# Layer 0 of a two-layer hybrid attention block: filler units four at a time with other VectorE steps behind each, all output projections first, and row sums one group later

## The chip, the cores and the metric

The kernel runs on one core of a Trainium2 chip. The metric is device time in microseconds (us), the median of three runs. Times quoted from the profile come from one profiled execution.

## What is computed

Two layers work on x of shape (2, 512, 64, 32), which is 2 batches of 512 channels and 2048 tokens, all in fp32. The change lies almost wholly in layer 0, whose reference, shortened, is:

```python
emb = get_embeddings(B, H, W, 32, 32)            # 32 frequency + 32 time channels
qk_hs = concatenate([hidden_states, emb], axis=1)   # 576 channels for q and k
q = qk_hs @ Wq
k = qk_hs @ Wk
v = v_hs @ Wv                                    # 512 channels for v
scores = einsum('bhqd,bhkd->bhqk', q, k) / sqrt(64)   # 8 heads of 64
attn = softmax(scores)
o = einsum('bhqk,bhkd->bhqd', attn, v)
x = o @ Wout + bout + hidden_states
```

Layer 1 takes a layer norm of this result per token, then attention by landmarks (256 landmarks, a pseudo-inverse by iteration), and then a second layer norm and a linear map whose weights are unpacked from 4-bit codes ("the feed-forward map"). The change touches the layer norm that stands at the head of layer 1, the place where the map's weights are unpacked, and one small function of layer 1.

## The kernel before

**Engines and order.** The instruction order on TensorE (PE), VectorE (DVE), ScalarE (ACT) and GpSimd (POOL) is the order in which the program issues them: these queues are scheduled by hand (L2070). Loads go out on SyncE's queue (SP). Stores of `x1_d` and `xh_d` go out on POOL's queue. A waiting instruction therefore holds up everything behind it on its engine.

**Layer 0's heads.** Heads are handled in pairs, `Heads0(b, hp)`: two batches with four pairs each, eight pairs in all, numbered n = 0 to 7 here and called "heads" below. For each, `attention0` (L1028) makes 64 steps (t, c): four blocks t of 512 queries, and for each 16 blocks c of 128 keys. Steps go in groups of two (GROUP = 2), at i = 0, 2, ... 64. For one group the program issues, in this order:

- the scores of its two steps on PE (L1040), in 64x64 tiles, into PSUM banks named "sc" (two of them), each followed by an exponential on ACT (L1048) into one of six SBUF tiles "p";
- two additions of p into `acc` on VectorE (L1058);
- the values of the group before it on PE (L1070), again in 64x64 tiles, into the banks av0 and av1 (one each); on the last key block of t, a copy of av0 on ACT (L1076) and an addition of av1 on VectorE (L1077) set the two banks free;
- some filler units (below);
- when a block t has ended, `sums` (L1080 and on): two row-sum matmuls of `acc` with ones on PE (`rs`, L1084), a reciprocal on VectorE (L1088) and the multiplication of the output by it on POOL (L1089).

**Filler units.** Between groups, PE works on generators. `advance(gens, n)` (L775) takes up to n units from a list of them, oldest first; a generator that yields GAP is passed over for this time. The units of the next head are: the embedding part of q (`fp`, a matmul of 96 columns L863, a VectorE copy `ft` L865, and an addition over 128x2048 on POOL, `e`, L867), four projections of q (four 128x512 matmuls each, L879, and the addition of `e` on VectorE, L882), the same for k, four units of v (16 matmuls each, L924, and an ACT copy L931), and last the reductions `big` on VectorE (2 x L912, L914). That is 15 units. In head 4 (b = 1, hp = 0) the list also holds `finish0_units` of batch 0: for each of four token blocks, a load of x, four output projections (`yp`, L939, with an addition on VectorE, L946), a store to `x1_d`, and the layer norm of the block, `norm0_steps`: partial sums on VectorE (`part`, L957 and L958), a mean matmul (L961), a subtraction (L962), two squares on ACT and two additions (L965 to L971), a variance matmul (L974), a square root on ACT, a reciprocal (L991), two multiplications (POOL L993, VectorE L994), and a store of `xh_d` (L995). Here the norm of one block is interleaved with the projections of the next. All of fp, pp, vp, yp, mean, var, and rs take turns in two PSUM banks ("pp").

**The steps beside.** `feed_forward_map` (L1113) unpacks the map's weights in 46 VectorE steps, most of them two pairs of operations (L1135, L1136), and ends in four PE units (`mp`). In heads 0 to 3 one step is taken in groups 1, 3 and 5 of every eight.

**How many fillers at a time.** With `due` as the share of the head's units that should have been made by group i, `attention0` takes two or three units when at least two are due; in head 4 (`every`) it takes one or two in every group. At the end of a head all units that are left of the next head are made.

**Start.** The first head's q, k and v are made before the first `attention0`. The weights and the embedding are loaded over SP, ACT's and POOL's queues (L803 to L815).

**`attend`** (layer 1, L1243) computes the scores of two landmark heads into the two halves of one PSUM tile `scs` (L1255) and exponentiates each into X on ACT (L1262), for pairs i = 0 to 2 of each batch; for i = 3 each half has a bank of its own.

Of the kernel before, what the change touches and what calls it, by code (L numbers as in the profile page):

```python
# [17 lines left out]
B, C, H, W = 2, 512, 64, 32  # L18
S = H * W
KC = C // P  # L20
# [641 lines left out]
def fast_path(  # L662
# [62 lines left out]
    def chunked(ap):  # L725
        return ap.rearrange("(k p) n -> p k n", p=P)
# [4 lines left out]
    def scores_bank(name):  # L731
        return ps.tile([P, 2, 512], F32, tag="sc", name=name)
# [18 lines left out]
    def block_of(pool, tag, name):  # L751
        return pool.tile([P, KC, TB], F32, tag=tag, name=name)
# [40 lines left out]
    def gap(n=1):  # L793
        for _ in range(n):
            yield GAP
# [5 lines left out]


    emb_sb = wpool0.tile([64, H + W], F32, name="emb_f")  # L803
    nc.vector.memset(emb_sb, 0.0)
    w_sb = {kind: wpool0.tile([P, KC, C], F32, name=f"w{kind}_f") for kind in "qk"}
    we = {kind: wpool0.tile([64, C], F32, name=f"we{kind}_f") for kind in "qk"}

    def load_w0(kind, cols, queue=nc.sync):
        w = {"q": wq0, "k": wk0}[kind]
        nc.sync.dma_start(w_sb[kind][:, :, cols], chunked(w[:C, cols]))  # L810
        queue.dma_start(we[kind][:, cols], w[C:, cols])

    nc.gpsimd.dma_start(emb_sb[:32, :H], freq)
    nc.gpsimd.dma_start(emb_sb[32:, H:], time)
    load_w0("q", slice(0, P), nc.scalar)  # L815

    def load_x(src, b, name, first=0, n=NTB):
        tiles = []
# [21 lines left out]
    class Heads0:  # L840
# [13 lines left out]
        def embedded_and_projected(self, kind):  # L854

            cols, xbs = self.cols, self.xbs
            if kind == "q":
                self.q = qopool.tile([P, S], F32, tag="qo", name=f"q_{self.name}")

            def embedded(kind):  # L860

                fp = bank(f"fp_{kind}_{self.name}")
                nc.tensor.matmul(fp[:, : H + W], lhsT=we[kind][:, cols], rhs=emb_sb, start=True, stop=True)  # L863
                ft = wpool0.tile([P, H + W], F32, tag="ft", name=f"ft_{kind}_{self.name}", bufs=2)
                nc.vector.tensor_copy(ft, fp[:, : H + W])  # L865
                e = wpool0.tile([P, H, W], F32, tag="e", name=f"e_{kind}_{self.name}")
                nc.gpsimd.tensor_tensor(  # L867
                    e,
                    ft[:, :H].unsqueeze(2).to_broadcast([P, H, W]),
                    ft[:, H:].unsqueeze(1).to_broadcast([P, H, W]),  # L870
                    ALU.add,
                )
                return e.rearrange("p h w -> p (h w)")

            def project(kind, dst, e, t):
                toks = slice(t * TB, (t + 1) * TB)
                pp = bank(f"pp_{kind}_{self.name}_{t}")
                for k in range(KC):
                    nc.tensor.matmul(  # L879
                        pp, lhsT=w_sb[kind][:, k, cols], rhs=xbs[t][:, k, :], start=k == 0, stop=k == KC - 1  # L880
                    )
                nc.vector.tensor_tensor(dst[:, toks], pp, e[:, toks], ALU.add)  # L882

            dst = self.q if kind == "q" else self.k
            e = embedded(kind)
            yield
            yield GAP
            for t in range(NTB):
                project(kind, dst, e, t)
                yield  # L890
# [104 lines left out]
        nc.gpsimd.dma_start(chunked(xh_d[b])[:, :, toks], xn)  # L995
        yield

    N_FINISH0 = NTB * (KC + 2)

    def finish0_units(b, oTs, outs_done):  # L1000
        last = None
        for t in range(NTB):
            xb = block_of(lpool, "xr", f"xr_f0_{b}_{t}")
            nc.sync.dma_start(xb, chunked(x[b])[:, :, t * TB : (t + 1) * TB])
            yield from gap()

            for m, _ in enumerate(out0_units(b, t, xb, oTs)):
                if last and m == 0:
                    next(last)
                yield  # L1010
            if t == NTB - 1:
                outs_done.append(True)
            if last:
                yield from gap()
            xn = block_of(lpool, "xn", f"xn_f0_{b}_{t}")
            last = norm0_steps(b, t, xb, xn, xn[:, :2, :])
            next(last)
            yield from gap(2)
            next(last)
            yield  # L1020
            yield from gap(2)
            next(last)
            yield from gap(2)
            next(last)
            yield
        next(last)

    def attention0(hd, filler, n_filler, needed, beside=None, every=False):  # L1028


        steps = [(t, c) for t in range(NTB) for c in range(NST)]
        av, acc, first, late = None, None, None, None

        def scores(t, c):
            sc = scores_bank(f"sc_{hd.name}_{t}_{c}")
# [56 lines left out]
        for i in range(0, len(steps) + 1, GROUP):  # L1092
            group = [(step, scores(*step)) for step in steps[i : i + GROUP]]
            for step, p in group:
                add(step, p)
            for step, p, its_acc in pending:
                values(step, p, its_acc)
            pending = [(step, p, acc) for step, p in group]
            due = n_filler * (i + GROUP) // len(steps)
            if every:  # L1100
                done += advance(filler, 2 if due - done >= 2 else 1)
            elif due - done >= 2:
                done += advance(filler, min(due - done, 3))
            if beside and i // GROUP % 8 in (1, 3, 5):
                advance(beside)
            if not group:
                while needed in filler:
                    advance(filler)
            if late:
                sums(*late)  # L1110
                late = None

    def feed_forward_map():  # L1113

# [68 lines left out]
    class Pair:  # L1183
# [59 lines left out]
        def attend(self):  # L1243

            i, L = self.i, self.L
            scs = scores_bank(f"sc2_{i}") if i + 1 < NPAIR else None
            X = self.X = [zpool.tile([P, 2, LM + 1], F32, tag=f"M{h}", name=f"X_{i}_{h}") for h in range(2)]
            rs = small.tile([P, 4], F32, tag="rs2", name=f"rs2_{i}")
            for h in range(2):
                nc.gpsimd.memset(X[h][:, :, LM:], 1.0)  # L1250
            for h in range(2):
                rows_h = slice(h * D, (h + 1) * D)
                sc = scs[:, h, :] if scs is not None else bank(f"sc2_{i}_{h}")
                for t in range(2):
                    nc.tensor.matmul(  # L1255
                        sc[:, t * LM : (t + 1) * LM],
                        lhsT=L[0][rows_h, t * P : (t + 1) * P],
                        rhs=L[1][rows_h, :],
                        start=True,
                        stop=True,  # L1260
                    )
                nc.scalar.activation(X[h][:, :, :LM], sc.rearrange("p (t n) -> p t n", n=LM), AF.Exp)  # L1262
            for h in range(2):
                two = slice(2 * h, 2 * h + 2)
                x_h = X[h][:, :, :LM]
                nc.vector.tensor_reduce(rs[:, two], x_h, AX.X, ALU.add)
                nc.vector.reciprocal(rs[:, two], rs[:, two])
                nc.vector.tensor_tensor(
                    x_h, x_h, rs[:, two].unsqueeze(2).to_broadcast([P, 2, LM]), ALU.mult
                )  # L1270
                nc.sync.dma_start(X_d[self.b, self.hp, h], x_h)
                nc.vector.tensor_reduce(rsum[:, i, two], x_h, AX.X, ALU.add)
# [405 lines left out]
    cur = Heads0(0, 0, xbs)  # L1678
    drain(cur.units())
    ffn_map = [feed_forward_map()]  # L1680
    oTs, finish, work = [], None, []
    for n, (b, hp) in enumerate(todo[:-1]):
        nb, nhp = todo[n + 1]
        if nb != b:
            xbs = load_x(x, nb, "x0")
        nxt = Heads0(nb, nhp, xbs)
        n_fill = Heads0.N_UNITS + 2 * len(work)
        if finish is None:
            units = nxt.units(wait=nb - b)
        else:  # L1690

            units = nxt.units(False, lambda: outs_done)
            work.append(finish)
            n_fill += N_FINISH0
        work.append(units)
        attention0(cur, work, n_fill, units, ffn_map if finish is None else None, finish is not None)
        finish = None
        oTs.append(cur.q)
        if n == 3:
            while ffn_map:  # L1700
                advance(ffn_map)
            wo_sb = load_wo(wo0, "wo_f0")
            write_bands()
        if hp == NPAIR - 1:
            outs_done = []
            finish = finish0_units(b, oTs, outs_done)
            oTs = []
        cur = nxt
    only0.close()


# [423 lines left out]
```

## Time and profile before

| | us |
|---|---|
| median of 3 runs | 2794.49 |
| lowest, highest run | 2793.27, 2799.08 |
| the profiled execution | 2797.65 |
| its span in the profile | 2795.8 |

The span runs from the first to the last instruction of the profile; the execution's own time has 1.85 us more around it. The profiled execution is 3.16 us over the median.

The eight heads of layer 0, as the windows of the trace show them (cut where PE begins the scores of a head):

| head | window, us | length | PE busy | DVE busy | POOL busy |
|---|---|---|---|---|---|
| 0 | 57.2 to 218.0 | 160.8 | 159.94 | 118.84 | 14.53 |
| 1 | 218.0 to 379.6 | 161.6 | 160.01 | 128.72 | 17.51 |
| 2 | 379.6 to 541.1 | 161.5 | 159.91 | 128.63 | 17.51 |
| 3 | 541.1 to 717.7 | 176.6 | 174.73 | 116.74 | 15.82 |
| 4 | 717.7 to 956.1 | 238.4 | 230.26 | 160.17 | 33.75 |
| 5 | 956.1 to 1117.5 | 161.4 | 160.16 | 110.89 | 20.82 |
| 6 | 1117.5 to 1277.8 | 160.3 | 159.91 | 107.92 | 16.66 |
| 7 | 1277.8 to 1421.9 | 144.1 | 143.81 | 107.06 | 9.65 |

A length less its PE busy time is the time that PE stood still, and in head 4 that is 8.1 us. PE busy time isn't PE at its peak: a change between kinds of matmul and a lower clock lengthen it as well. Head 3 holds the 16 `mp` matmuls, and head 4 the output projections of batch 0.

### The profile page before, as it was taken

To read this page: it belongs to the slowest core of one execution; us is meant where nothing else is said; L and a number is where in the kernel's file an instruction comes from. 1 tells how busy PE (TensorE), PEld (TensorE's weight loads), DVE (VectorE), ACT (ScalarE), POOL (GpSimd) and SP (SyncE) were. 2 spreads that over 40 slices of the span, in tenths; PEclk is the share of its full clock that TensorE was granted. 3 is DMA by queue.
4 is the path that set the end of the run, shared out by engine and by line. 5 is a ranking of instruction groups with operands and counts; after the bars stand their busy time and mean duration, and the time that the engine had idled before them with its cause. 6 is when DMAs were issued, how large, how long until landed. Compare 5 with 4: busy or idle time off the path is not lost.

```text
span 2795.8 us, 39629 instructions
## 1 busy us (share of the span) xinstructions
PE 2736.7 (98%) x16754; PEld 1374.5 (49%) x16754; DVE 1776.0 (64%) x2111; ACT 913.5 (33%) x1352; POOL 231.6 (8%) x130
## 2 busy tenths in 40 slices
PE   9999999999999999999999999999999999999899
PEld 5343443434443334344334455777677666555334
DVE  2868788784658775767757544446755745566475
ACT  1434343433234334434422223223323323221210
POOL 1101101010101210100002000001000100000000
PEclk9999999999999999999999999999999999999999
DMA  3000000101001200002025532302101102110201
GB/s 114 5 5 1 5 1 1 61 16 46 27 31 61 76 1 1 1 31 68 16 79 175 196 126 91 104 30 77 65 28 51 44 22 82 41 43 19 98 23 46
DMA packets 85770, 140.31 MB, mean 50 GB/s; under 512 B 7872, under 2 KB 43216, under 8 KB 83024
## 3 DMA queue, kind: packets, MB, share of 16 engines
q1 hardware_dynamic: 81088, 120.87, 13.0%
q0 software_dynamic: 4416, 16.79, 1.6%
q8 instruction: 133, 2.18, 0.3%
q14 instruction: 53, 0.43, 0.1%
q10 hardware_dynamic: 80, 0.03, 0.0%
HBM read 82.48 MB, written 55.19 MB: 49 GB/s over the span
## 4 chain that ended last, share of the span: by engine, by line
PE 87%; DVE 9%; ACT 1%; issue 1%; DMA 1%; POOL 0%; DVEq 0%; SPq 0%; ACTq 0%; POOLq 0%
PE sc_f L1040 13%; PE av_f L1070 13%; PE pp L1214 8%; PE pb L1507 5%; PE pa L1507 5%; PE vp_f L924 4%; PE vp L924 4%; PE pp_k_f L879 4%; PE fp_g L1658 4%; DVE acc_f L1058 4%; PE yp_g L939 3%; PE yp_f L939 3%; PE pp_q_f L879 3%; PE sc L1564 2%; PE sc L1336 2%; PE av L1357 2%
## 5 line engine op out<-in xcount | busy, mean ns | idle before, releaser
L1058 DVE TENSOR_TENSOR acc_f<-acc_f,p_f 128x1024 f32<-128x1024 f32 x448 | 611.3, 1365 | 217.8 <-ACT p_f L1048 188.8
L1048 ACT ACTIVATE p_f<-sc_f 128x1024 f32<-128x1024 f32 x512 | 496.8, 1022 | 580.2 <-PE sc_f L1040 574.0
L1040 PE MATMUL sc_f<-q_f,k_f 64*64 64x512 f32 x4096 | 491.7, 595 | 2.9 <-ACT p_f L1048 2.9
L1070 PE MATMUL av_f<-p_f,v_f 64*64 64x512 f32 x4096 | 484.3, 589 | 0.0
L1070 PEld LDWEIGHTS av_f<-p_f,v_f 64*64 64x64 f32 x4096 | 156.5, 133 | 283.1 <-issue 283.1
L1040 PEld LDWEIGHTS sc_f<-q_f,k_f 64*64 64x64 f32 x4096 | 144.7, 133 | 293.9 <-issue 253.1
L1214 PE MATMUL pp<-xh,w 128*128 128x512 f32 x512 | 231.3, 604 | 0.7 <-ACT q L1217 0.7
L1214 PEld LDWEIGHTS pp<-xh,w 128*128 128x128 f32 x512 | 96.0, 192 | 122.1 <-issue 114.9
L1507 PE MATMUL pb<-R 128*128 128x192 f32 (+1 forms) x640 | 152.5, 385 | 1.6 <-DVE M L1520 1.6
L1507 PE MATMUL pa<-M 128*128 128x192 f32 (+1 forms) x640 | 150.6, 380 | 0.0
L1089 POOL TENSOR_TENSOR q_f<-q_f,rinv_f 128x512 f32<-128x512 f32 x32 | 68.4, 2137 | 825.5 <-DVE rinv_f L1088 825.5
L1596 DVE RECIPROCAL acc<-acc 128x256 f32<-128x256 f32 x64 | 111.3, 1743 | 28.0 <-ACT acc L1591 28.0
L1602 POOL TENSOR_TENSOR o<-o,acc 128x512 f32<-128x512 f32 x32 | 53.6, 1674 | 872.6 <-DVE acc L1601 837.2
L924 PEld LDWEIGHTS vp_f<-wv_f,x 128*128 128x128 f32 x1024 | 115.6, 192 | 12.7 <-issue 11.0
L879 PE MATMUL pp_q_f<-x,wq_f 128*128 128x512 f32 x256 | 116.9, 609 | 4.5 <-DVE q_f L882 3.1
L1507 PEld LDWEIGHTS pb<-R 128*128 128x128 f32 x640 | 108.7, 194 | 25.4 <-DVE M L1520 2.5
L924 PE MATMUL vp<-w,xh 128*128 128x128 f32 x1024 | 120.8, 276 | 0.0
L924 PEld LDWEIGHTS vp<-w,xh 128*128 128x128 f32 x1024 | 117.0, 192 | 7.2 <-issue 4.2
L939 PE MATMUL yp_f<-q_f,wo_f 128*128 128x512 f32 x256 | 115.9, 606 | 4.2 <-DVE rinv_f L1088 3.3
L924 PE MATMUL vp_f<-wv_f,x 128*128 128x128 f32 x1024 | 118.5, 276 | 0.0
L1507 PEld LDWEIGHTS pa<-M 128*128 128x128 f32 x640 | 108.0, 193 | 21.0 <-ACT M L1498 2.5
L939 PE MATMUL yp_g<-o,wo_f 128*128 128x512 f32 x256 | 115.5, 598 | 0.8 <-ACT p L1569 0.8
(202 smaller groups left out, 3000.4 us busy)
## 6 DMA issues: line engine op xcount, KB each, us to landing
xh<-xh_fd SPq DMA_DIRECT2D x12, 1024.0 KB, 5.4
xr_f<-in_x_dram SPq DMA_DIRECT2D x8, 1024.0 KB, 5.0
x_fd<-xr_f POOLq DMA_DIRECT2D x8, 1024.0 KB, 4.8
xh_fd<-xn_f POOLq DMA_DIRECT2D x8, 1024.0 KB, 4.6
k_fd<-k SPq DMA_DIRECT2D x32, 256.0 KB, 2.8
q_fd<-q SPq DMA_DIRECT2D x32, 256.0 KB, 3.1
xb_g<-x_fd SPq DMA_DIRECT2D x32, 256.0 KB, 4.7
k<-k_fd SPq DMA_DIRECT2D x8, 1024.0 KB, 5.7
```

Source lines behind the costliest of these rows:

```text
L879: nc.tensor.matmul(pp, lhsT=w_sb[kind][:, k, cols], rhs=xbs[t][:, k, :], start=k == 0, stop=k == KC - 1)
L924: nc.tensor.matmul(vp[:, j * P : (j + 1) * P], lhsT=xb[:, k, j * P : (j + 1) * P], rhs=w_of(k), start=k == 0, stop=k == KC - 1,)
L939: nc.tensor.matmul(yp, lhsT=wo_sb[:, k, m * P : (m + 1) * P], rhs=oTs[k][:, toks], start=k == 0, stop=k == NPAIR - 1,)
L1040: nc.tensor.matmul(sc[r * D : (r + 1) * D, h, :], lhsT=hd.k[rows, lo : lo + D], rhs=hd.q[rows, t * TB : (t + 1) * TB], start=True, stop=True,)
L1048: nc.scalar.activation(p, sc, AF.Exp, scale=D**-0.5)
L1058: nc.vector.tensor_tensor(acc, first if c == 1 else acc, p, ALU.add)
L1070: nc.tensor.matmul(av[r][half, :], lhsT=hd.v[keys, c, half], rhs=pp[keys, h, :], start=c == 0, stop=c == NST - 1,)
L1089: nc.gpsimd.tensor_tensor(o, o, rinv, ALU.mult)
L1214: nc.tensor.matmul(pp, lhsT=self.w[j][:, c, :], rhs=xhs[t][:, c, :], start=c == 0, stop=c == KC - 1)
L1507: nc.tensor.matmul(dst, lhsT=lhsT[:, k, t * P : (t + 1) * P], rhs=rhs[:, k, :], start=k == 0, stop=k == 1)
L1596: nc.vector.reciprocal(half, half)
L1658: nc.tensor.matmul(fp[:, cols], lhsT=mT[:, k, m * P : (m + 1) * P], rhs=self.xn[:, k, cols], start=k == 0, stop=k == KC - 1,)
```

## The change

1. **Start.** The embedding tile is cleared in two parts that don't overlap what is loaded into it; the first q weights and the embedding are all loaded over ACT's queue, in the order wq, weq, freq, time; the first head's two additions `e` go to VectorE instead of POOL.
2. **Four at a time.** `attention0` takes fillers in bursts of four calls once four are due (a call that finds only a GAP counts as one of the four). Behind every unit made it takes one step of `beside`, also at the end of a head. For batch 0's heads `beside` is the feed-forward map, for batch 1's it is the new `norm0_units`.
3. **Row sums a group later.** `sums` of a block t is issued one group after the group whose values ended it.
4. **Projections first.** `finish0_units` makes the output projections of all four blocks, with x loaded one block ahead into two tiles in turn. The layer norm moves to `norm0_units`, which loads the blocks again from `x1_d` and is taken as `beside` in heads 4 and later.
5. **`attend`.** Each of the two heads has a PSUM tile of its own, and the column of ones in X is set by VectorE instead of POOL.

```diff
--- before.py
+++ after.py
@@ -801,18 +801,19 @@
     emb_sb = wpool0.tile([64, H + W], F32, name="emb_f")
-    nc.vector.memset(emb_sb, 0.0)
+    nc.vector.memset(emb_sb[:32, H:], 0.0)
+    nc.vector.memset(emb_sb[32:, :H], 0.0)
     w_sb = {kind: wpool0.tile([P, KC, C], F32, name=f"w{kind}_f") for kind in "qk"}
     we = {kind: wpool0.tile([64, C], F32, name=f"we{kind}_f") for kind in "qk"}
     def load_w0(kind, cols, queue=nc.sync):
         w = {"q": wq0, "k": wk0}[kind]
-        nc.sync.dma_start(w_sb[kind][:, :, cols], chunked(w[:C, cols]))
+        queue.dma_start(w_sb[kind][:, :, cols], chunked(w[:C, cols]))
         queue.dma_start(we[kind][:, cols], w[C:, cols])
-    nc.gpsimd.dma_start(emb_sb[:32, :H], freq)
-    nc.gpsimd.dma_start(emb_sb[32:, H:], time)
     load_w0("q", slice(0, P), nc.scalar)
+    nc.scalar.dma_start(emb_sb[:32, :H], freq)
+    nc.scalar.dma_start(emb_sb[32:, H:], time)
     def load_x(src, b, name, first=0, n=NTB):
         tiles = []
@@ -864,7 +865,9 @@
                 ft = wpool0.tile([P, H + W], F32, tag="ft", name=f"ft_{kind}_{self.name}", bufs=2)
                 nc.vector.tensor_copy(ft, fp[:, : H + W])
                 e = wpool0.tile([P, H, W], F32, tag="e", name=f"e_{kind}_{self.name}")
-                nc.gpsimd.tensor_tensor(
+                engine = nc.gpsimd if self.b or self.hp else nc.vector
+                engine.tensor_tensor(
                     e,
                     ft[:, :H].unsqueeze(2).to_broadcast([P, H, W]),
                     ft[:, H:].unsqueeze(1).to_broadcast([P, H, W]),
@@ -995,41 +998,40 @@
         nc.gpsimd.dma_start(chunked(xh_d[b])[:, :, toks], xn)
         yield
-    N_FINISH0 = NTB * (KC + 2)
     def finish0_units(b, oTs, outs_done):
-        last = None
+        def load(t):
+            xb = block_of(lpool, ("xr", "xn")[t % 2], f"xr_f0_{b}_{t}")
+            nc.sync.dma_start(xb, chunked(x[b])[:, :, t * TB : (t + 1) * TB])
+            return xb
+        nxt = load(0)
+        yield from gap()
         for t in range(NTB):
-            xb = block_of(lpool, "xr", f"xr_f0_{b}_{t}")
-            nc.sync.dma_start(xb, chunked(x[b])[:, :, t * TB : (t + 1) * TB])
-            yield from gap()
-            for m, _ in enumerate(out0_units(b, t, xb, oTs)):
-                if last and m == 0:
-                    next(last)
+            xb = nxt
+            if t + 1 < NTB:
+                nxt = load(t + 1)
+            yield from out0_units(b, t, xb, oTs)
+        outs_done.append(True)
+    def norm0_units(b, outs_done):
+        while not outs_done:
+            yield
+        for t in range(NTB):
+            xb = block_of(lpool, "xr", f"x1_f0_{b}_{t}")
+            nc.sync.dma_start(xb, chunked(x1_d[b])[:, :, t * TB : (t + 1) * TB])
+            yield
+            xn = block_of(lpool, "xn", f"xn_f0_{b}_{t}")
+            for _ in norm0_steps(b, t, xb, xn, xn[:, :2, :]):
                 yield
-            if t == NTB - 1:
-                outs_done.append(True)
-            if last:
-                yield from gap()
-            xn = block_of(lpool, "xn", f"xn_f0_{b}_{t}")
-            last = norm0_steps(b, t, xb, xn, xn[:, :2, :])
-            next(last)
-            yield from gap(2)
-            next(last)
-            yield
-            yield from gap(2)
-            next(last)
-            yield from gap(2)
-            next(last)
-            yield
-        next(last)
-    def attention0(hd, filler, n_filler, needed, beside=None, every=False):
+    def attention0(hd, filler, n_filler, needed, beside=()):
         steps = [(t, c) for t in range(NTB) for c in range(NST)]
-        av, acc, first, late = None, None, None, None
+        av, acc, first, late, ended = None, None, None, None, None
         def scores(t, c):
             sc = scores_bank(f"sc_{hd.name}_{t}_{c}")
@@ -1097,18 +1099,22 @@
                 values(step, p, its_acc)
             pending = [(step, p, acc) for step, p in group]
             due = n_filler * (i + GROUP) // len(steps)
-            if every:
-                done += advance(filler, 2 if due - done >= 2 else 1)
-            elif due - done >= 2:
-                done += advance(filler, min(due - done, 3))
-            if beside and i // GROUP % 8 in (1, 3, 5):
-                advance(beside)
+            for _ in range(4 if due - done >= 4 else 0):
+                made = advance(filler)
+                if made and beside:
+                    advance(beside)
+                done += made
             if not group:
                 while needed in filler:
                     advance(filler)
-            if late:
-                sums(*late)
-                late = None
+                    if beside:
+                        advance(beside)
+                ended = late
+            if ended:
+                sums(*ended)
+            ended, late = late, None
     def feed_forward_map():
@@ -1243,14 +1249,14 @@
         def attend(self):
             i, L = self.i, self.L
-            scs = scores_bank(f"sc2_{i}") if i + 1 < NPAIR else None
+            scs = [scores_bank(f"sc2_{i}_{h}")[:, 0, :] for h in range(2)] if i + 1 < NPAIR else None
             X = self.X = [zpool.tile([P, 2, LM + 1], F32, tag=f"M{h}", name=f"X_{i}_{h}") for h in range(2)]
             rs = small.tile([P, 4], F32, tag="rs2", name=f"rs2_{i}")
             for h in range(2):
-                nc.gpsimd.memset(X[h][:, :, LM:], 1.0)
+                nc.vector.memset(X[h][:, :, LM:], 1.0)
             for h in range(2):
                 rows_h = slice(h * D, (h + 1) * D)
-                sc = scs[:, h, :] if scs is not None else bank(f"sc2_{i}_{h}")
+                sc = scs[h] if scs else bank(f"sc2_{i}_{h}")
                 for t in range(2):
                     nc.tensor.matmul(
                         sc[:, t * LM : (t + 1) * LM],
@@ -1678,7 +1684,7 @@
     cur = Heads0(0, 0, xbs)
     drain(cur.units())
     ffn_map = [feed_forward_map()]
-    oTs, finish, work = [], None, []
+    oTs, finish, work, norm = [], None, [], []
     for n, (b, hp) in enumerate(todo[:-1]):
         nb, nhp = todo[n + 1]
         if nb != b:
@@ -1691,10 +1697,10 @@
             units = nxt.units(False, lambda: outs_done)
             work.append(finish)
-            n_fill += N_FINISH0
+            n_fill += NTB * KC
+            finish = None
         work.append(units)
-        attention0(cur, work, n_fill, units, ffn_map if finish is None else None, finish is not None)
-        finish = None
+        attention0(cur, work, n_fill, units, norm if b else ffn_map)
         oTs.append(cur.q)
         if n == 3:
             while ffn_map:
@@ -1704,8 +1710,11 @@
         if hp == NPAIR - 1:
             outs_done = []
             finish = finish0_units(b, oTs, outs_done)
+            next(finish)
+            norm.append(norm0_units(b, outs_done))
             oTs = []
         cur = nxt
+    assert not norm
     only0.close()
```

## The prediction

> **What bounds the kernel now.** I read the shares of busy time first, then the chain of waits, then PE's waits in layer 0, then the timeline where the change touches.
>
> ```profile
> PE 2736.7 (98%) x16754; PEld 1374.5 (49%) x16754; DVE 1776.0 (64%) x2111; ACT 913.5 (33%) x1352; POOL 231.6 (8%) x130
> PE 87%; DVE 9%; ACT 1%; issue 1%; DMA 1%; POOL 0%; DVEq 0%; SPq 0%; ACTq 0%; POOLq 0%
> ```
>
> PE sets the end. Any gain has to be PE time: waits, a low clock, or changes between kinds of matmul. PE's waits up to 1425 us, where layer 0's heads end, are:
>
> ```profile
> PE rs_f L1084 <- DVE acc_f L1058: 3.8, 4, 1.2
> PE pp_q_f L879 <- DVE q_f L882: 3.1, 1, 3.1
> PE sc_f L1040 <- ACT p_f L1048: 2.9, 8, 0.9
> PE mean_n L961 <- DVE xn_f L958: 2.8, 1, 2.8
> PE yp_f L939 <- DVE rinv_f L1088: 2.4, 1, 2.4
> PE var_n L974 <- DVE xr_f L971: 1.6, 1, 1.6
> ```
>
> The numbers are total, times, longest. Little is left: some 20 us of 1425. The price of going to a filler and back isn't a wait; it is in the timeline of PE:
>
> ```profile
> 79.00 1.90 PE L1070 MATMUL av_f<-p_f,v_f 64*64 64x512 f32 x16
> 80.83 7.13 PE L879 MATMUL pp_q_f<-x,wq_f 128*128 128x512 f32 x16
> 87.89 1.95 PE L1040 MATMUL sc_f<-q_f,k_f 64*64 64x512 f32 x16
> 89.66 1.90 PE L1070 MATMUL av_f<-p_f,v_f 64*64 64x512 f32 x16
> ```
>
> From start to start, the values take 1.83 us here against 1.72 elsewhere (75.57 to 77.29), the projections 7.06 against 16 x 0.429 = 6.86, and the scores 1.77 against 1.72: 0.11 + 0.20 + 0.05 = 0.36, say 0.37 us per visit. Next, a GpSimd addition and VectorE's:
>
> ```profile
> 287.68 5.80 DVE L1058 TENSOR_TENSOR acc_f<-acc_f,p_f 128x1024 f32<-128x1024 f32 x2
> 287.89 4.51 POOL L867 TENSOR_TENSOR e_k_f<-ft_k_f 128x2048 f32<-128x2048 f32 x1 [24.88 <-DVE ft_k_f L865]
> ```
>
> Two additions take 2.55 us just before (285.03); here 5.80, the second alone 4.47 from 289.01. Last, the start:
>
> ```profile
> 14.99 3.62 POOL L867 TENSOR_TENSOR e_q_f<-ft_q_f 128x2048 f32<-128x2048 f32 x1 [11.58 <-issue]
> 18.65 1.29 DVE L882 TENSOR_TENSOR q_f<-pp_q_f,e_q_f 128x512 f32<-128x512 f32 x2 [9.66 <-POOL e_q_f L867]
> 19.39 4.97 PE L879 MATMUL pp_q_f<-x,wq_f 128*128 128x512 f32 x7 [3.15 <-DVE q_f L882]
> ```
>
> Weight loads come every 0.85 us from 20.39 to 22.91 instead of 0.43: PE ran at half its clock for 3.4 us after the stop. The same is seen at 726.0 and 941.05, after stops of 2.36 and 2.83, not after stops up to 1.7. Each costs 1.7 us beyond the stop.
>
> [...]
>
> **The change, part by part.** The instruction orders before and after give the positions.
>
> *Start.* `e` for q on VectorE begins once `ft` is there (9.0 us) instead of on POOL at 14.99. By the 2.28 us of the subtraction at L962, the same 128x2048, it is done at about 11.5, before the first projection ends. So the stop of 3.15, its half clock of 1.7 and the first 0.2 of embedding wait go: -5.0. The unknown is when the embedding lands, now behind a 256 KB weight load on ACT's queue; the warm-up matmuls cover it until 8.03. Bounds -6 and 0.
>
> *Visits.* Filler visits in layer 0's attention (row sums apart, 29 alone in both) fall from 76 to 37: by head 8, 8, 8, 10, 22, 8, 8, 4 become 4, 4, 4, 5, 9, 4, 4, 3. 39 x 0.37 = -14.4.
>
> *Waits that go.* Row sums 3.8 (VectorE has 3.4 us more), yp on rinv 2.4, mean 2.8, var 1.6, yp on xr 0.8, pp on xr 0.5, pp on `ft` 0.7, exponentials at the start of head 5 about 0.9: 13.5, and two half clocks (726.0, 941.05), 3.4: -16.9.
>
> *New waits.* A group takes PE 3.43 us, VectorE about 2.6, ACT 2.04, so VectorE gains only 0.8 us per group on a backlog, and a burst makes one:
>
> - Heads 0, 1, 2, visit at i = 28: two projections, then fp of k, with a map step (about 2.2 us: two pairs of 0.42 + 0.69) behind each, [...]. VectorE comes out about 5 us late. Next in its order is the addition that frees av1 (L1077, i = 32), so PE stops at the values of i = 34, by my sum for 2.7, 3.4 and 3.75 us (head 0 began with less behind it), each with a half clock: 9.85 + 5.1 = +15.0. Bounds 0 (VectorE recovers) and +30.
> - Ends of heads 0, 1: two map steps (3.3 us) stand between `big` and the reciprocal; the six p tiles run out for 1.0 and 1.1: +2.1.
> - End of head 4: the norm of block 2 begins with `part` on VectorE, which waits until the store of block 1 has landed (5.05 us after POOL's multiplication, as at 931.75 to 936.80). The mean matmul stops PE for 3.3, plus 1.7. Then block 2's squares stand on ACT before head 5's first exponential, and wait for the subtraction, which is behind the av addition and `big`: 7.5, plus 1.7. Together +14.2. Bounds 0 and +25.
> - Heads 4 and 5: squares (2 x 1.06) in the last unit of a visit delay exponentials, 1.6 twice; the values 1.7, the mean 1.2, a PSUM bank 0.55: +6.7.
> - End of head 7: the last projection now comes after the last values, row sums and rinv follow: +0.8.
>
> Sum of new waits: +38.8. Moved DMAs: four more 1 MB reads of `x1_d` on SP (5.0 us each) and the earlier x loads lie beside idle queues (DMA share 0.14 in head 4); the x1 stores on POOL now stand before later `e` operations by their issue of 0.75 us only: nothing. The `mp` units move from head 3 to head 2: nothing.
>
> *attend.* At 1455.17, 1522.53 and 1561.72 the two scores take 2.92, 5.66 and 4.37 us from start to start of what follows, against 1.07 where two banks are used (1599.39). The line is
>
> ```profile
> PE sc L1255 <- ACT X L1262: 6.2, 3, 3.5
> ```
>
> Excess 9.7 us, and half clocks at 1528.19 and 1566.09 worth 3.3: 13.0. In the second the variance matmul right behind needs an addition (L971) that ends at 1530.88 whatever PE does, so of its share I keep 1 of 6.3. With 1.2 of 1.85 and 4.8 of 4.8: -7. Bounds -11 and -2. The 128x2 memset on VectorE is priced below 0.2.
>
> *Sum.* -5.0 - 14.4 - 16.9 + 38.8 - 7.0 = -4.5; by head, n = 0 to 7: +2.3, +3.3, +3.8, -3.2, -8.5, +10.7, -1.5, +0.4 = +7.3, with the start and attend -4.7. I take -4.7. On the profiled 2797.65 that is 2792.9; on the median, 3.2 lower, **2789.8**.
>
> **Rivals.** A difference of 0.2%, 5.6 us, is about what a measurement of this kernel can tell from no change.
>
> - *VectorE recovers* (faster). If av1 and the exponentials are never late, +15.0, +2.1 and +6.7 go: 2789.8 - 23.8 = 2766. For it: DVE is 74 to 80% busy in heads 0 to 2, and PE's order leaves one group of slack. Against it: row sums waited 1.2 us in heads 1 and 2 even with one map step at a time.
> - *Start lost, attend small* (no change): embedding late, +5.0, attend -5 instead of -7: 2797, within 0.2% with a little luck elsewhere.
> - *The lock decides* (slower). Place: the visit at i = 28 of heads 0 to 2. POOL's `e` there meets not one VectorE addition but several, [...] (569.2 shows a map addition at 4.00 instead of 0.69). If it costs a second lock per head, the stop is 6 to 7 us and may cost a second half clock: 3.3 + 1.7 = 5.0 more per head, 15 in all: 2805. It decides from 1.6 us per head (no gain) and makes the kernel slower beyond 0.2% from 3.4 per head (10.3 over three heads). Against it: `e` is one instruction, [...].
>
> **How the numbers follow.** Forecast as worked out, within about 6 us: 0.40. VectorE recovers, wholly or by half: 0.22. Start lost: 0.13. The lock, or the end of head 4 at its upper bound: 0.25. The forecast lies near the 0.2% line, so it gives faster 0.20, same 0.19, slower 0.01; recovery faster 0.22; start lost same 0.11, slower 0.02; the lock same 0.02, slower 0.23. Sum: faster 0.42, same 0.32, slower 0.26. Range for 8 in 10: from half of the recovery with some more (2772) to short of the lock's full price (2804).
>
> **What would show it.** Start: `e_q` on VectorE near 9 us, no stop at 16 to 19. Visits: heads 3 and 6 shorter by 1.5 to 3. Backlog: in heads 0 to 2 a wait "av on DVE q" of about 3 us, three times, with half clock after it. End of head 4: scores waiting for exponentials behind ACT's squares, 7 us. attend: the line of L1255 gone, and the wait at 1522 now at var. Wrong if heads 0 to 2 are shorter than before (recovery), if their stops exceed 6 us (the lock), or if fp of q waits for the embedding.

## The result, and the profile after

Over twelve runs each, taken by turns, the changed kernel took 2795.86 us in the median (2790.22 to 2800.16) and the kernel before 2796.72 (2793.27 to 2799.39). The ratio is 0.9997, with a 95% interval of 0.9989 to 1.0005: no change that can be measured. The forecast of -4.7 us lies just outside that interval (-3.1 to +1.4). The profiled execution of the changed kernel took 2800.16 us, the slowest of the twelve; its span is 2798.7 against 2795.8 before.

The lengths, cut as before at the first scores of each head:

| stretch | before | after | difference | forecast |
|---|---|---|---|---|
| start to head 0 | 57.2 | 53.0 | -4.2 | -5.0 |
| head 0 | 160.8 | 161.8 | +1.0 | +2.3 |
| head 1 | 161.6 | 168.4 | +6.8 | +3.3 |
| heads 2 and 3 | 338.2 | 342.5 | +4.3 | +0.6 |
| head 4 | 238.4 | 228.2 | -10.2 | -8.5 |
| head 5 | 161.4 | 174.0 | +12.6 | +10.7 |
| head 6 | 160.3 | 159.1 | -1.2 | -1.5 |
| from the first scores of head 7 to the end | 1517.9 | 1511.7 | -6.2 | -6.6 |

Heads 1 to 3 hold 7.2 of the 7.6 us by which the profiled execution missed the forecast. PE's waits up to 1425 us are now (total, times, longest):

```profile
PE sc_f L1042 <- ACT p_f L1050: 12.7, 12, 5.7
PE av_f L1072 <- DVE q_f L1079: 7.7, 4, 2.7
PE mean_n L964 <- DVE xn_f L961: 3.2, 2, 2.5
PE pp_q_f L882 <- DMA x<-in_x_dram: 1.8, 1, 1.8
PE mp L1154 <- DMA wff_f<-in_wffT_dram: 1.4, 1, 1.4
PE rs_f L1086 <- DVE acc_f L1060: 1.3, 1, 1.3
```

The list of before had row sums, q on the addition of `e`, mean, rinv and var. Of these the changed list keeps 1.3 us of row sums and has a mean wait at another place. Two large lines stand at its head: scores on exponentials, which grew from 2.9 us to 12.7, and values on the addition that frees av1, which is new. Head 1's backlog, in VectorE's timeline:

```profile
284.39 0.25 DVE L866 COPY ft_k_f<-fp_k_f 128x96 f32<-128x96 f32 x1
284.56 0.41 DVE L1131 CAST tmp_f<-tmp_f 128x512 f32<-128x512 int32 x1
285.00 3.75 DVE L1133 TENSOR_SCALAR hits_f<-tmp_f 128x512 f32<-128x512 f32 x1
288.79 0.69 DVE L1134 TENSOR_TENSOR tmp_f<-tmp_f,hits_f 128x512 f32<-128x512 f32 x1
...
293.14 1.22 DVE L1060 TENSOR_TENSOR acc_f<-p_f,p_f 128x1024 f32<-128x1024 f32 x1
294.28 0.68 DVE L1079 TENSOR_TENSOR q_f<-av_f,q_f 128x512 f32<-128x512 f32 x1
```

The map step behind `fp` of k meets POOL's `e` (3.68 us from 284.78): L1133, which takes 0.43 us in its three other places, takes 3.75. The addition L1079 ends at 294.96, and PE's values start at 295.01 after a stop of 2.59. What comes then is in the table of windows (length, PE busy, PE's granted clock, DMA):

```profile
290.60:294.00 3.40, 1.83 (x16) 1.00 0.01 2
294.00:297.40 3.40, 2.38 (x10) 0.50 0.00 0
297.40:300.80 3.40, 3.40 (x12) 0.50 0.00 0
300.80:304.20 3.40, 3.40 (x20) 0.50 0.00 0
304.20:307.60 3.40, 3.40 (x39) 0.99 0.02 5
```

The half clock lasts three windows, 10.2 us. From start to start, 16 scores take 3.46 us in them (300.53 to 303.99) and 1.72 behind them (305.85 to 307.57). PE was busy for 9.2 of the 10.2, and by that ratio I estimate half of the 9.2, 4.6 us, as lost; the time in which PE stood still is counted as no loss. Losses by half clock below are estimated in the same way. All three of layer 0's half clocks before lasted one window. In heads 0, 1 and 2 there are 0, 3 and 2 windows, at the end of head 4 there are 3.

The end of head 4, VectorE, ACT and PE in turn:

```profile
947.92 1.23 DVE L960 TENSOR_TENSOR xn_f<-x_f 128x1024 f32<-128x1024 f32 x1 [5.03 <-DMA xh_fd<-xn_f]
```

```profile
959.75 1.06 ACT L968 ACTIVATE x_f<-xn_f 128x1024 f32<-128x1024 f32 x1 [11.66 <-DVE xn_f L965]
960.71 1.04 ACT L971 ACTIVATE x_f<-xn_f 128x1024 f32<-128x1024 f32 x1
961.66 1.92 ACT L1050 ACTIVATE p_f<-sc_f 128x1024 f32<-128x1024 f32 x2
```

```profile
949.92 1.12 PE L964 MATMUL mean_n<-xn_f,mean_w 128*128 128x512 f32 x2 [2.46 <-DVE xn_f L961]
952.39 1.61 PE L1086 MATMUL rs_f<-acc_f,ones 128*64 128x512 f32 x4 [1.34 <-DVE acc_f L1060]
...
962.71 3.69 PE L1042 MATMUL sc_f<-q_f,k_f 64*64 64x512 f32 x16 [5.73 <-ACT p_f L1050]
```

VectorE stood 5.03 us for the store of the block before, so mean and row sums were late; then the exponentials of head 5 stood on ACT behind two squares, the first of which waited for the subtraction (11.66 us idle on ACT, until 959.75). This is the chain that the prediction had named.

### The profile page after: what moved, and what is told of

The parts are those of the page before. It is cut to its first block, busy times and chain, and to the rows that moved or that the text cites. A ratio compares the mean times of both kernels' runs of the same rounds, so it can differ in the third digit from the quotient of the medians.

```text
span 2798.7 us, 39626 instructions
## 1 busy us (share of the span) xinstructions
PE 2730.6 (98%) x16754; PEld 1376.4 (49%) x16754; DVE 1769.0 (63%) x2130; ACT 915.5 (33%) x1354; POOL 215.6 (8%) x110
## 4 chain that ended last, share of the span: by engine, by line
PE 90%; DVE 5%; DMA 2%; issue 1%; ACT 1%; POOL 0%; SPq 0%; DVEq 0%; ACTq 0%; POOLq 0%
PE av_f L1072 15%; PE sc_f L1042 15%; PE pp L1220 8%; PE pb L1513 5%; PE pa L1513 5%; PE vp L927 4%; PE vp_f L927 4%; PE fp_g L1664 4%; PE pp_q_f L882 4%; PE yp_f L942 4%; PE pp_k_f L882 4%; PE yp_g L942 3%; PE sc L1570 2%; PE sc L1342 2%; PE av L1363 2%; PE av L1586 2%
## 5 line engine op out<-in xcount | busy, mean ns | idle before, releaser
L1060 DVE TENSOR_TENSOR acc_f<-acc_f,p_f 128x1024 f32<-128x1024 f32 x448 | 579.9, 1294 | 189.5 <-ACT p_f L1050 155.5
L1042 PE MATMUL sc_f<-q_f,k_f 64*64 64x512 f32 x4096 | 495.8, 600 | 12.7 <-ACT p_f L1050 12.7
L1072 PE MATMUL av_f<-p_f,v_f 64*64 64x512 f32 x4096 | 492.1, 592 | 7.7 <-DVE q_f L1079 7.7
L1072 PEld LDWEIGHTS av_f<-p_f,v_f 64*64 64x64 f32 x4096 | 159.1, 134 | 296.3 <-issue 282.5
```

The costliest lines, as they stand in the source:

```text
L1042: nc.tensor.matmul(sc[r * D : (r + 1) * D, h, :], lhsT=hd.k[rows, lo : lo + D], rhs=hd.q[rows, t * TB : (t + 1) * TB], start=True, stop=True,)
L1060: nc.vector.tensor_tensor(acc, first if c == 1 else acc, p, ALU.add)
L1072: nc.tensor.matmul(av[r][half, :], lhsT=hd.v[keys, c, half], rhs=pp[keys, h, :], start=c == 0, stop=c == NST - 1,)
```

## The experiments

The theory at the outset: bursts do save visits, but VectorE and ACT come out of them late, and the stops that this makes on PE, with their half clocks, eat what was saved. The rivals: the bursts save nothing, or the stops come from elsewhere. Every lone run beside is one execution; what is compared is the lengths of stretches in the trace.

**The start alone.** The kernel before with part 1 of the change.

> The kernel before with part 1 alone (cleared halves, ACT's queue, the first two additions e on VectorE). Theory (the parts add up, the start is worth what the two traces show): the scores of head 0 begin at about 53.0 us instead of 57.2, no stop of 3.15 and no half clock near 19, and the eight heads keep their lengths of before within 0.5 us each. Rival (the start only lends its time, since the x blocks or weights are late next): the scores begin after 55.5.

Scores of head 0 began at 55.2 us, between the theory's 53.0 and the rival's 55.5; the heads kept their lengths within 0.4. The stop of 3.15 is gone, but PE now stops 1.93 us for an x block at 13.9, and in this execution a half-clock window (1.7 us lost) began at 14.6. The ten other traces with this start, those below and the changed kernel's, begin head 0 between 51.7 and 53.1. With the old start head 0 began at 57.2 in the kernel before and at 56.2 in the next run, where the stop for `e`, 3.29 us there, dropped no clock. So the start is worth 3 to 5.5 us, and less in the one execution in which a half clock came with the stop for x (2.0, from 57.2 to 55.2).

**attend alone.** The kernel before with part 5.

> The kernel before with part 5 alone (a bank for each of attend's two heads, ones set by VectorE). Theory: the time from the last scores of head 7 to the end is 1379 to 1380 us, as in the changed kernel, against 1385.5 before, and layer 0 is as before. Rival (those 5.9 us came from what layer 0 left behind in head 7's end, not from attend): 1384 or more.

The time from the last scores of head 7 to the end was 1378.7 us, against 1385.5 before and 1379.6 in the changed kernel. The theory holds: attend's gain is its own. Its size is less sure than one execution makes it look: in the eleven traces with part 5 this stretch took 1375.7 to 1381.1 us, in the two without it 1385.5 and 1386.4.

**The map's steps at their old places.**

```diff
-                if made and beside:
+                if made and beside and hd.b:
                     advance(beside)
...
+            if beside and not hd.b and i // GROUP % 8 in (1, 3, 5):
+                advance(beside)
             if not group:
                 while needed in filler:
                     advance(filler)
-                    if beside:
+                    if beside and hd.b:
                         advance(beside)
```

> The changed kernel, but the feed-forward map's steps in heads 0 to 3 stand where they stood before (groups 1, 3 and 5 of eight), not behind the units. Theory (VectorE's backlog behind the burst with fp of k, and the half-clock windows that its stop starts, ate the gain): the stops of av on the addition L1079 at i = 34 go or stay under 1 us, no half-clock window in heads 0 to 2, heads 0, 1 and 2 take 158.5 to 160 each apart from the map's own matmuls, against 161.8, 168.4 and 183.2 (with the map's matmuls). Rival 1 (the addition e on POOL alone, at the end of the burst, makes VectorE late): stops of 2 us or more remain and heads 1 and 2 gain less than 2 us. Rival 2 (bursts save nothing per visit): heads 0 to 2 come to 160.8 to 161.6, as before.

Heads 0 to 3 took 159.1, 160.9, 160.9 and 177.3 (now with the map's matmuls in head 3): 658.2 together, against 672.7 changed and 660.5 before. No av stop and no half clock is left there:

```profile
PE pp_q_f L882 <- DVE ft_q_f L866: 3.0, 2, 1.5
PE pp_q_f L882 <- DVE q_f L885: 2.4, 1, 2.4
PE sc_f L1042 <- ACT p_f L1050: 1.1, 4, 0.3
```

So the map's steps behind the units cost 14.5 us over four heads, 8.0 of it by half clock, and `e` on POOL alone makes no stop of av. Heads 1 and 2 come out 0.9 over the range expected: the embedding copy, in the first burst, now waits for a map step (238.40 to 240.60 in head 1) that VectorE's additions were still catching up with.

**Nothing beside at the end of a head.**

```diff
                 while needed in filler:
                     advance(filler)
-                    if beside:
-                        advance(beside)
```

> The changed kernel, but no step of other work is taken behind the units at the end of a head. Theory (the end of head 4 is late by the norm's steps there): the waits of 2.46, 1.34 and 5.73 us at 949.9 to 962.7 and their three half-clock windows go, heads 4 and 5 together take about 387 to 391 us against 402.2, and the waits of 0.87 and 1.42 at the start of heads 1 and 2 go. Rival (the norm's work is only moved and stops PE at a later visit instead): heads 4 and 5 together stay over 397.

The waits at the start of heads 1 and 2 went, as expected. But heads 4 and 5 took 406.2 us together against 402.2: the rival was right. PE's waits from 900 to 1125 us:

```profile
PE av_f L1072 <- DVE q_f L1079: 6.5, 2, 5.4
PE rs_f L1086 <- DVE acc_f L1060: 5.0, 1, 5.0
PE sc_f L1042 <- ACT p_f L1050: 1.8, 3, 1.3
```

Behind both large stops VectorE stands in `part` for the store of the block before, 5.10 us (until 937.63) and 6.58 us (until 1022.62). In both kernels the wait for the store stands where the next block's first step stands (5.03 us at 947.92 in the changed one).

**Row sums at once.** Part 3 undone.

```diff
-            if ended:
-                sums(*ended)
-            ended, late = late, None
+            if late:
+                sums(*late)
+                late = None
```

> The changed kernel, but row sums come at once as before (part 3 undone). Theory (VectorE is late after the burst with fp of k, whatever waits for it): at i = 32 the row sums of heads 0, 1 and 2 wait for the additions, 3 us or more each, in place of the stops of av at i = 34, and heads 0 to 2 take 1 to 4 us more each than in the changed kernel. Rival (part 3 is worth nothing): heads 0 to 2 within 1 us of 161.8, 168.4 and 183.2 once half-clock windows are taken off.

Row sums stopped PE for 2.50, 3.42 and 3.57 us in place of av's 1.67, 2.59 and 2.73: VectorE's backlog stopped whatever needed it first. With the half clock's loss taken off, heads 0 to 2 took 161.5, 165.0 and 180.4 here, and 161.8, 163.7 and 179.8 in the changed kernel. The waits moved as the theory says, the first of them under its 3 us; the lengths lie between it and the rival, about 0.5 us per head for part 3, from one execution of each.

**Head 4 as before.** Part 4 undone: `finish0_units` with the norm in it, one or two units in each group of head 4.

```diff
+            if every:
+                done += advance(filler, 2 if due - done >= 2 else 1)
+                due = done
             for _ in range(4 if due - done >= 4 else 0):
...
-        attention0(cur, work, n_fill, units, norm if b else ffn_map)
+        attention0(cur, work, n_fill, units, () if b else ffn_map, finish is not None)
+        finish = None
```

> The changed kernel with part 4 undone: in head 4 the projections and the norm of batch 0 stand and are taken as before (one or two units in every group), and nothing is taken behind the units of batch 1. Theory (projections first saves visits in head 4 but gives it back at its end and in head 5): heads 4 and 5 together take 397 to 400 us, 2 to 5 less than the changed kernel's 402.2. Rival (projections first is a gain by itself): 404 or more.

Heads 4 and 5 took 235.3 + 160.2 = 395.5 us, 6.7 less than changed, 4.3 less than before, and under the 397 to 400 expected. Projections first, as it stands in the change, is a loss. Heads 0 to 3 hold the same program here as in the changed kernel, so this run (a_head4) is a second sample of their stops, used below.

**What sets the length of a half clock.** The prediction had charged each stop with one window. Two kernels changed what follows the stop at i = 34: `a_exit` puts the burst of k's projections straight behind the values there (run twice), `a_sums2` takes the row sums one group further away.

```diff
-            for _ in range(4 if due - done >= 4 else 0):
+            early = not hd.b and hd.hp < 3
+            for _ in range(4 if (i in (34, 58) if early and i > 30 else due - done >= 4) else 0):
```

> The changed kernel, but in heads 0 to 2 the burst of the four k projections comes at i = 34, straight behind the values that stop for av, instead of at i = 42, and the v burst stays at i = 58. Theory (after a stop the half clock lasts two or three windows of 3.41 us because 64x64 matmuls follow it; with 128x128 matmuls it lasted one in the kernel before): the stops at i = 34 stay near 2.6 us, and where one starts a half clock it lasts one window, or two if the window ends before the projections begin, 1.7 to 3.4 us lost instead of up to 5.1. Rival (the length is set by the stop, not by what follows): three windows again in one of the heads 1 and 2, two in the other.

> The kernel of a_exit once more, for a second sample of where the windows of the clock fall. Theory (128x128 projections end a half clock after one window): each half clock that the stops of heads 1 and 2 start lasts one window, two if the first holds 0.8 us or more of the stop. Rival (the one window of a_exit was chance): two or three without that.

```diff
-            ended, late = late, None
+            ended, soon, late = soon, late, None
```

> The changed kernel, but row sums come two groups later instead of one, so that scores and values follow the stop at i = 34 and the row sums come only behind them. Theory (a window at half clock is followed by another if it holds 0.8 us or more of the stop, or values and row sums together): a half clock in head 1 or 2 lasts one or two windows, never three, and heads 1 and 2 are 1.5 to 4 us shorter than the changed kernel's 168.4 and 183.2. Rival (any 64x64 work behind a stop keeps the half clock for two or three windows): three windows in one of them, or two where no part of the stop lies in the first.

The stops stayed as they were (2.58 and 2.73 us, within 0.01). Their half clocks did not, and they differ between executions of one program too:

| kernel | windows in heads 0, 1, 2 | heads 1 and 2, us |
|---|---|---|
| changed | 0, 3, 2 | 168.4, 183.2 |
| a_head4, the same program in these heads | 0, 2, 3 | 166.7, 184.2 |
| a_exit | 0, 0, 1 | 163.7, 181.3 |
| a_exit_b | 0, 2, 2 | 167.0, 183.0 |
| a_sums2 | 1, 0, 1 | 163.9, 181.5 |

For a_sums2 the theory's expectation held; the trace's windows around head 2's stop (PE, PEld, DVE, ACT, POOL busy, then the clock):

```profile
458.20:461.60 3.40, 1.31 (x12) 0.55 (x16) 3.30 (x5) 0.00 (x0) 0.00 (x0) 1.00 0.00 0
461.60:465.00 3.40, 3.40 (x20) 1.28 (x16) 1.10 (x1) 0.51 (x1) 0.00 (x0) 0.50 0.00 0
465.00:468.40 3.40, 3.40 (x28) 0.96 (x24) 2.45 (x2) 1.54 (x2) 0.00 (x0) 1.00 0.00 0
```

Here the one window at half clock held 2.62 us of scores. For a_exit_b the expectation fell:

```profile
293.60:297.00 3.40, 3.30 (x12) 0.77 (x12) 2.40 (x3) 0.00 (x0) 0.00 (x0) 0.50 0.00 0
297.00:300.40 3.40, 3.40 (x6) 1.51 (x5) 0.00 (x0) 0.00 (x0) 0.00 (x0) 0.50 0.00 0
300.40:303.80 3.40, 3.40 (x9) 1.46 (x8) 1.11 (x3) 0.00 (x0) 0.00 (x0) 0.99 0.00 0
```

The first window was nearly full, but of values alone (3.33 us), and a second followed, with the projections in it, before the clock was full again. So neither "64x64 against 128x128" nor the length of the stop is the rule. In the 76 half-clock windows of the thirteen traces up to 1800 us one regularity is left, found afterwards and not tested as such: a half-clock window was followed by another if 0.8 us or more of it was idle, or if it held values, row sums or both, and at most about 0.4 us of other matmuls; a window with more of scores or of 128x128 matmuls was the last. The windows nearest to these limits: 0.81 us idle was followed by another (a_head4, 293.7) and 0.57 was not (a_exit_b, 959.2); 0.41 us of scores beside values and row sums was followed (the run with nothing beside at the end of a head, 1031.3) and 0.51 was not (a_head4, 297.1). Why the limit for values is another than for scores of the same tile size was not shown. What the traces have beside it is that part of the values behind such a stop start two at a time instead of four (in a_exit_b four at 293.70 and 294.61, two at 295.46 and 296.32). What is shown is that one stop of about 2.6 us costs between nothing and 4.6 us of clock, and not the same in each execution of a program; the part that the work behind it plays is read off afterwards.

**A mended version.** `a_best` keeps all five parts but chooses where the steps beside go: for the map behind two q units and the k and v units only, for the norm in two halves per block in separate bursts, so that the next block's `part` comes at least one burst after the store.

```diff
+    HOLD = object()
+    BEHIND = (0, 0, 1, 1, 0, 0, 1, 1, 1, 1, 1, 2, 1, 2, 0, 0)
...
-            yield
+            yield HOLD
...
-            for _ in norm0_steps(b, t, xb, xn, xn[:, :2, :]):
-                yield
+            for j, _ in enumerate(norm0_steps(b, t, xb, xn, xn[:, :2, :])):
+                if j < 4:
+                    yield HOLD if j == 1 else None
...
+            held = False
             for _ in range(4 if due - done >= 4 else 0):
                 made = advance(filler)
-                if made and beside:
-                    advance(beside)
+                if made and beside and hd.b and not held:
+                    got = next(beside[0], beside)
+                    held = got is HOLD
+                    if got is beside:
+                        beside.pop(0)
+                if made and not hd.b:
+                    advance(beside, BEHIND[done])
                 done += made
             if not group:
                 while needed in filler:
                     advance(filler)
-                    if beside:
-                        advance(beside)
```

> A mended version: the changed kernel, but the map's steps stand behind the units of k and v and behind two of q, none behind the last units before or at fp and none at the end of a head, and the norm of a block is taken in two halves: partial sums and mean in one burst, squares, variance and scaling in the next, so that no VectorE step waits for a store of xh that has just been issued. Theory (VectorE and ScalarE lateness behind the bursts is what ate the gain): heads 0 to 2 about 159 us each, head 3 about 175, heads 4 and 5 together 384 to 390, no half-clock window in layer 0 or one at most, and about 30 us less than the kernel before in all (0.988 to 0.990). Rival (VectorE has no room anywhere, so the stops only move): over 2785 us, or 0.996 and more.

It took 2768.24 us, 0.9901 of the kernel before (0.9885 to 0.9918). Heads 0 to 6 took 159.1, 159.1, 159.1, 173.0, 219.9, 168.2 and 165.0, with one half-clock window in layer 0. Its waits up to 1425 us:

```profile
PE var_n L977 <- DVE x_f L974: 6.2, 2, 3.1
PE sc_f L1046 <- ACT p_f L1054: 2.3, 8, 0.3
PE yp_f L942 <- DVE rinv_f L1094: 1.8, 1, 1.8
```

Neither the av stops nor the exponentials' large stop is left, and the time is near what the theory had: 28 us faster by the medians instead of about 30. In the profiled executions heads 0 to 6 hold 17 of it; most of the rest is the start and attend. This shows that the bursts are worth having once the work beside them is placed: heads 0 to 2 take 159.1 each, against 160.8 to 161.6 before. For the new order of projections and norm it isn't shown: heads 4 to 6 take 553.1 us together here, and 554.6 in "Head 4 as before", which does without it. The last run tried to clear the line of var.

```diff
                     yield HOLD if j == 1 else None
+                if j == 2:
+                    yield
```

> The mended version a_best with one more unit between the squares and the variance matmul of the norm. Theory (the stops of 3.1 us before var in heads 5 and 6 come from the addition of the squares, which the addition e on POOL holds up to 3.75 us instead of 1.22): both stops and the half-clock window at 1129 go, heads 5 and 6 are shorter by 3 us or more each, and the time is 0 to 8 us under a_best's 2768.2. Rival (the variance now stands last in its burst, so ScalarE's change of tables for the square root stands before the next exponentials and stops PE there instead): heads 5 and 6 within 3 us of 168.2 and 165.0 together, time within 3 us of a_best.

The var stops of 3.1 us went (0.65, for ACT, is left in head 4), but PE stopped for mean (2.77), exponentials (0.86), av (1.71) and row sums (1.66) instead, and a half clock of two windows came at 1167.8. Heads 5 and 6 took 336.8 us against 333.2, and the time was 2770.80 (0.9912, 0.9896 to 0.9929): the rival was right that they would not gain, but its cause, the exponentials, makes only 0.86 us of these stops. The change of tables that the rival names took 1.28 us each way in the changed kernel's trace (931.67, ahead of the square root, and 933.67, ahead of the exponentials). Why the stops moved there in each case I did not follow up.

## Why the prediction was right or wrong

- **Start, -5.0; measured -4.2.** The addition on VectorE ran at 8.36 to 10.65 as priced. Not foreseen: PE then stops 1.82 us for an x block. The prediction had asked only what the embedding would do, and for that PE waited just 0.5.
- **Visits, -14.4.** Head 6, where little else changed, lost 1.2 us for four visits: 0.30 each instead of 0.37, so -11.7 for 39. In a_best heads 0 to 2 PE was busy 158.8 us each, against 159.9 to 160.0 before, which is about the same per visit.
- **Waits that go, -16.9.** All of them went; the 1.3 us of row sums that are left belong to the new chain at the end of head 4.
- **av stops in heads 0 to 2, +15.0.** Place, cause and order were right. The stops were 1.67, 2.59 and 2.73, 7.0 instead of 9.85. The step that failed is "each with a half clock", one window of 1.7 each: it was none, three and two windows, which cost 0, 4.6 and 3.4, 8.0 us instead of 5.1. The sum, 15.0, meets the forecast by luck, since the two errors cancel; head 0's share was smaller, head 1's larger. In other runs it is another sum: a_exit and a_sums2 lost 1.7 and 3.4 us to the clock in heads 0 to 2.
- **Ends of heads 0 and 1, +2.1; measured 0.87 + 1.42 = 2.3.**
- **End of head 4, +14.2.** Measured 2.46 + 1.34 + 5.73 and 3.6 for three windows: 13.1. Three windows don't cost three times 1.7 here: the second began at 959.6, and PE stood still in it until 962.71. The prediction's 1.7, half of 3.4, is the estimate for a window in which PE is busy throughout.
- **Heads 4 and 5 besides, +6.7; measured** 1.34 twice, 0.66 and 0.76: 4.1.
- **The map's matmuls, nothing.** Wrong by 1.35: PE waits for their weights, whose load is issued at 494.16, only 4 us before they are needed.
- **attend, -7.0; measured -5.9.** The second pair's stop moved to the variance matmul (3.69 at 1539.1, where before it was 3.48 at 1527.1), and its half clock with it, as priced. With the spread of that stretch ("attend alone"), -7.0 can't be told from -5.9.

The end of head 7 came as priced: rinv stops PE 1.80 us there, against 0.95 before. By these terms the sum moves by +0.8 + 2.7 + 0.0 + 0.2 - 1.1 - 2.6 + 1.4 + 1.1 = +2.5 of the 7.6. A further part is a cost that the prediction put at nothing: an av stop takes more than its wait. Head 0 in the changed kernel, and then in a_best, where nothing stops:

```profile
128.41 1.03 PE L1072 MATMUL av_f<-p_f,v_f 64*64 64x512 f32 x4
131.11 1.93 PE L1072 MATMUL av_f<-p_f,v_f 64*64 64x512 f32 x12 [1.67 <-DVE q_f L1079]
132.98 1.08 PE L1086 MATMUL rs_f<-acc_f,ones 128*64 128x512 f32 x4
```

```profile
128.39 1.90 PE L1076 MATMUL av_f<-p_f,v_f 64*64 64x512 f32 x16
130.22 1.08 PE L1090 MATMUL rs_f<-acc_f,ones 128*64 128x512 f32 x4
```

From the first value to the row sums it is 4.57 us against 1.83, so a stop of 1.67 cost 2.74. It lies in the midst of a group's values, when av0 is free and av1 isn't yet: four of the sixteen start two at a time before it (128.41, 128.84), and four more behind it (132.02, 132.45), where a_best has four at a time. In heads 0 to 2 this comes to 1.1, 1.2 and 1.3 us, 3.6 in all; in each head that is about what four visits less save. The remaining 1.5 us isn't assigned. By the medians over twelve runs the miss is 3.8 us; the profiled execution was one with much half clock (mean granted clock 0.990, the lowest of the twelve). The rivals: recovery didn't come by itself, and its time, 28.5 us under the kernel before, is about what a_best reached by placing the work otherwise; at the visit at i = 28 of heads 0, 1 and 2 one VectorE operation beside POOL's `e` took 3.3 us longer (4.01 us instead of 0.69, 3.75 instead of 0.43, 4.01 instead of 0.69), and no second one did. That extra time is all that the traces show of what the prediction calls the lock.

## What to carry to other kernels

A filler unit on the busiest engine brings work to the engines beside it; place that work by what each of them must deliver next, not by counting units. The costly places here were beside POOL's `e`, where one VectorE operation took 3.3 us longer, and right behind a store, for which VectorE stood 5.03 us with the rest of its work behind the wait. Price a stop on PE as a range: its length (here 1.67 to 2.73 us in heads 0 to 2), the sets of tiles that it breaks up (1.1 to 1.3 us), and the time lost in none to three windows of half clock (0 to 4.6 us by the estimate above).

## What the runs showed of the hardware

- The windows of the clock lie on a grid of 3.413 us in the changed kernel's trace: its half clocks up to 1600 us began at 294.0, 464.7, 952.8, 959.6 and 1539.9, which are 50, 143, 2 and 170 times 3.413 apart. The one at 294.0 followed a window (290.6 to 294.0) with 1.60 us of stop. A half clock came with the stop of 1.67 us in head 0 in a_sums2, and not in the changed kernel.
- Much of the spread between runs goes with the clock: of the changed kernel's twelve, the three with a mean granted clock of 0.990 took 2799.2 to 2800.2 us, the three with 0.993 took 2791.7 to 2794.6, and the one with 0.995 took 2790.2.
- Beside POOL's `e`, additions of two tensors took longer in the changed kernel's trace (L1142 at 122.84 and 454.76, 4.01 us against 0.69), and so did an operation of one tensor and a scalar (L1133 at 285.00, 3.75 us against 0.43).
